# Turning the second half of a normalised input by DMA in a two-layer graph kernel

## The chip, the cores and the metric

The kernel runs on one core of a Trainium2 chip. The metric is device time in microseconds (us) of one execution. Engines are called PE (TensorE, matrix products), DVE (VectorE), ACT (ScalarE), POOL (GpSimd) and SP (SyncE, which here issues every DMA, in one queue and in program order). Each engine works through its own instructions in order and waits for others by semaphores.

## The reference, cut to what matters

The input x has 128 elements of 128 nodes by 512 features. Layer 0 is a graph convolution; layer 1 is masked attention of eight heads. Both begin with a layer normalisation and a ReLU, and both add their result to x.

```
# layer 0
h = relu(layernorm(x))
x = x + norm_adj @ (h @ weight) + bias
# layer 1
h = relu(layernorm(x))
q, k, v = h @ Wq + bq, h @ Wk + bk, h @ Wv + bv        # 8 heads of 64
attn = softmax(q k^T / 8 + (1 - adj) * -1e9)
x = x + (attn v) @ Wo + bo
```

The change concerns the h of layer 1: it stands node by feature after the normalisation and is needed feature by node, as operand of the three products q, k and v.

## The kernel before, in words

**Groups and stages.** The 128 elements are worked in 32 groups of four (`GB = 4`, `NG = 32`). A stage t has five blocks: W (layer 0's product for group t+1), Q, K and V (the three projections of group t), Y (the output projection of group t-1). Each block has seven steps, `W0` to `W6` and so on, one for each of seven block products in a Strassen-like scheme (`PRODUCTS`, lines 31 to 39), split once more inside; the sums of operands that the scheme needs are made on POOL (`combine`, `combine_one`), and DVE and ACT add the products from the accumulator banks into the result (`add` at line 440, `read` at 455, the copies at 770 and 784). PE's order is thus fixed: P1, P5, P2, P6, P3, P7, P4 in every block.

**The plan.** All other work is put between the steps by hand: `at(t, "V2", f, ...)` runs f just before step V2 of stage t, "V2b" comes after the step's matmuls and first reads, and "V2c" after the rest. Nothing is reordered afterwards, so the place of a call is its place in the queue of each engine that it uses, SP's queue too.

**The normalised input of layer 1 (h).** For group g = t+1, `norm_h(g, b)` (line 715, an activation at 344) makes h of element b in a tile of a pool of two. Elements 0 and 1 go by DMA: `split_h` (736) copies the fp32 words on ACT into two planes of 16 bits, in an attention buffer that is free at the time; after element 1 the planes are written to DRAM (743) and `turn_h` (745) reads them back with a transposing DMA (748) into the first eight slots of `op_norm`, blocks A11 and A12. Elements 2 and 3 go by PE: `transpose_h` (719) makes sixteen 64-row transposes for each into a bank (730), and ACT copies the bank into blocks S1 and A22 (731). Both are in stage t: `norm_h` at V1, V2, V5, V6; `split_h` at V2b and V3, `turn_h` at Y0, `transpose_h` at Y1 and Y2. `attention_operands` at Y5 starts POOL's sums over all four blocks (373 to 376, then 94); Q of the next stage reads them.

**The attention planes** go the same way as elements 0 and 1 of h: `split_att` (850) writes planes (854), `turn_att` (856) reads them back transposed (857), for elements 0 to 3 of the group before; elements 2 and 3 are needed by `attend` at V0.

**Other transfers in SP's queue.** x of group t+2 is loaded in two halves (`load_x`, 170): the first half at W2 into a buffer that a store (897) must first have left, the second at W5, just behind `turn_att` of element 0. `ln1` needs the second half at Q3b: DVE takes its statistics (325), and behind them in DVE's order stand reads of Q's banks. Four of the five weights stream through two buffers, each in four parts of 11, 11, 11 and 7 slots (`PARTS`, `reload_w`, 1063): `reloads_of` (1065) lists the places, and in its row "W" the V weights come at W6, Q4, Q1 and K3; the part of Q4 holds W22 and T3, which V4 and V5 read.

Of the kernel before, what the change touches and what calls it, by code (L numbers as in the profile page):

```python
# [9 lines left out]
U16 = mybir.dt.uint16  # L10
# [17 lines left out]
A11, A12, S1, A22, S2, S3, S4 = range(7)  # L28
# [17 lines left out]
LEFT_AT = {A11: 0, A12: 4, S1: 8, A22: 12, S2: 16, S3: 20, S4: 24}  # L46
# [51 lines left out]
def kernel(  # L98
# [16 lines left out]
    nc = tc.nc  # L115
    B, N, D = x.shape
    P = 128
    H = 8
    HD = D // H
    NC = D // P  # L120
    GB = 4
    NG = B // GB
# [4 lines left out]
    dp = ctx.enter_context(tc.tile_pool(name="dp", bufs=1, space=bass.MemoryType.DRAM))  # L127
# [27 lines left out]


    planes_dram = [dp.tile([P, 2, H * P], U16, tag=f"planes_{b}", name=f"planes_{b}") for b in range(GB)]
    h_dram = dp.tile([P, 2, H * P], U16, tag="planes_h", name="planes_h")
    adj_sb, an = (att_buf[2][:, i, :] for i in range(2))
    bias_part = att_buf[4][:, 0:NC, :].rearrange("p c f -> p (c f)")  # L160
    ones = att_buf[4][:, NC, :]
# [222 lines left out]
    op_mix, op_norm, op_att = (Operands(f"op_{k}") for k in "aho")  # L384
# [250 lines left out]
    hs = {}  # L635
# [83 lines left out]
    def transpose_h(g, b):  # L719
# [13 lines left out]
            pt.bitcast(U16).rearrange("p (z c n) -> p c n z", z=2, c=NC),  # L733
        )

    def split_h(g, b):


        h2 = hs.pop((g, b)).bitcast(U16).rearrange("n (c f z) -> n z c f", c=NC, z=2)
        planes = att_of(g - 1, -1).bitcast(U16).rearrange("n h k -> n (h k)")  # L740
        nc.scalar.copy(planes.rearrange("n (z c j f) -> n z c j f", z=2, c=NC, j=2)[:, :, :, b, :], h2)
        if b == 1:
            nc.sync.dma_start(h_dram, planes.rearrange("n (z f) -> n z f", z=2))

    def turn_h(g):
        op_h[g] = op_norm
        blocks = op_norm.t.bitcast(U16)[:, LEFT_AT[A11] : LEFT_AT[A11] + 8, :]
        nc.sync.dma_start_transpose(out=blocks, in_=h_dram.rearrange("n z f -> (n z) f"))

    def attention_operands(g):  # L750
        op_h[g].combine(nc.vector if g < 2 else nc.gpsimd, g > 0, within=nc.gpsimd)
# [5 lines left out]
    qs, ks, vs = {}, {}, {}  # L757
# [36 lines left out]
    def att_of(g, b):  # L794


        return att_buf[(b - g) % (GB + 1)]
# [106 lines left out]
    def at(slot, place, f, *args):  # L904
        plan.setdefault((slot, place), []).append((f, *args))

    for t in range(-1, NG + 1):
# [3 lines left out]
        if 0 <= t - 1 < NG - 1:  # L911
            g = t - 1
# [27 lines left out]
        if t == 0:  # L940

            at(0, "Q0b", ln2, 1, 0)
            at(0, "Q1b", ln2, 1, 1)
            at(0, "K6", norm_h, 1, 0)
            at(0, "K6", norm_h, 1, 1)
            at(1, "W0", transpose_h, 1, 0)
            at(1, "W0", norm_h, 1, 2)
            at(1, "W1", transpose_h, 1, 1)
            at(1, "W1", norm_h, 1, 3)
            at(1, "W2", transpose_h, 1, 2)  # L950
            at(1, "W3", transpose_h, 1, 3)
            at(1, "W4b", attention_operands, 1)
            at(2, "Q5", attention_residual, 1, 0)
            at(2, "K1", attention_residual, 1, 1)
        elif 1 <= t + 1 < NG and t >= 0:
            g = t + 1
            at(t, "K0b" if g < NG - 1 else "Q0b", ln2, g, 0)
            at(t, "K6b" if g < NG - 1 else "Q3b", ln2, g, 1)
            if g == NG - 1:

                places = ("Q3", "Q4", "Q5", "Q5", "Q6", "Q6", "K1", "K2", "K2")
                steps = ((norm_h, 0), (norm_h, 1), (transpose_h, 0), (norm_h, 2), (transpose_h, 1), (norm_h, 3))
                steps += ((transpose_h, 2), (transpose_h, 3))
            else:
                places = ("V1", "V2", "V2b", "V3", "V5", "V6", "Y1", "Y2", "Y5")
                steps = ((norm_h, 0), (norm_h, 1), (split_h, 0), (split_h, 1), (norm_h, 2), (norm_h, 3))
                steps += ((transpose_h, 2), (transpose_h, 3))
                at(t, "Y0", turn_h, g)
            for place, (f, b) in zip(places, steps):
                at(t, place, f, g, b)  # L970
            at(t, places[8], attention_operands, g)
            at(t + 1, "Q3", attention_residual, g, 0)
            at(t + 1, "Q4", attention_residual, g, 1)
# [6 lines left out]
        if 2 <= t + 2 < NG:  # L980
            g = t + 2
# [4 lines left out]
            places = (("Q3", "Q5"), ("Q4", "Q6"), ("Q5b", "K1"), ("Q6", "K2"))  # L986
# [6 lines left out]
        if 0 <= t < NG:  # L993
            g = t
            for b in (0, 1, 3, 2):
                at(t, "V0", scores, g, b)
            if t > 0:
                at(t, "V0", output_operands, t - 1)
            at(t, "V1b", row_max, g, 0)
            at(t, "V3b", exponentials, g, 0, 0, H // 2)  # L1000
            at(t, "V4b", exponentials, g, 0, H // 2, H)
            at(t, "V6", softmax_end, g, 0)
            if last:
                at(t, "V5b", row_max, g, 1)
                at(t, "V5b", exponentials, g, 1, 0, H // 2)
                at(t, "V6", exponentials, g, 1, H // 2, H)
                at(t, "Y1b", softmax_end, g, 1)
                at(t, "Y2", transpose_att, g, 0)
                at(t, "Y4", transpose_att, g, 1)
            else:  # L1010
                if t > 0:
                    at(t, "V3b", row_max, g, 1)
                    at(t, "Y1", exponentials, g, 1, 0, H // 2)
                    at(t, "Y2", exponentials, g, 1, H // 2, H)
                    at(t, "Y4", softmax_end, g, 1)
                else:
                    at(t, "V4b", row_max, g, 1)
                    at(t, "V5b", exponentials, g, 1, 0, H // 2)
                    at(t, "V6", exponentials, g, 1, H // 2, H)
                    at(t + 1, "W1b", softmax_end, g, 1)  # L1020
                at(*((t, "Y3b") if t > 0 else (1, "W1")), split_att, g, 0)
                at(t, "V6b", row_max, g, 2)
                at(*((t, "Y1") if t > 0 else (1, "W0")), add_mask, g, 3)
                at(*((t, "Y3b" if g == NG - 2 else "Y6b") if t > 0 else (1, "W4b")), row_max, g, 3)
        if last:
            g = t
# [38 lines left out]
    def reloads_of(t):  # L1065

        when = {
            "W": ((t, "W6"), (t, "Q4"), (t, "Q1"), (t, "K3")),
            "Q": ((t, "K4"), (t, "K6"), (t, "V0"), (t, "V1")),
            "V": ((t, "V3"), (t, "Y0"), (t, "Y1"), (t, "Y3")),  # L1070
            "Y": ((t, "Y5"), (t + 1, "W0"), (t + 1, "W0"), (t + 1, "W3" if t + 1 < NG - 1 else "Q5")),
        }
        if t == 1:

            when["Q"] = ((1, "K3"),) * 4
        for kind in "WQVY":
            if kind == "W" and t + 1 == NG or kind in "QV" and t == NG:
                continue
            reading[0] += 1
            for part, place in enumerate(when[kind]):  # L1080
                at(*place, reload_w, reading[0] + 2, part)
# [89 lines left out]
    with tc.manual_schedule(  # L1171
        engines={
            mybir.EngineType.PE,
            mybir.EngineType.DVE,
            mybir.EngineType.Activation,
            mybir.EngineType.Pool,
            mybir.EngineType.SP,
        }
    ):
        prologue()  # L1180
        for t in range(1, NG + 1):
            reloads_of(t)

        for t in range(NG + 1):
            if t > 0:
                block(t, "W", t + 1, gcn_weight)
            if t < NG:
                block(t, "Q", t, lambda g: qk(g, 0))
                block(t, "K", t, lambda g: qk(g, 1))
                block(t, "V", t, values)  # L1190
            block(t, "Y", t - 1, attention_out)
            if 0 < t < NG:
                store_half(t - 1, 0)
            elif t == NG:
                store_half(t - 1, 1, slice(0, 256))
# [41 lines left out]
```

## Time and profile before

| what | value |
|---|---|
| three timed executions | 2237.06, 2238.38 and 2242.81 us, median 2238.38 |
| the profiled execution's own time | 2240.26 us, of it 2238.5 us span |
| busy in the span | PE 2218.4 us, POOL 1867.5, DVE 1799.0, ACT 1387.1 |
| DMA | 565.15 MB in 448,697 packets; 326,352 packets under 512 B |
| issues | 150 transposing DMAs (121 of attention, 29 of h), 121 + 29 writes of planes, 484 weight parts and a few more |
| granted PE clock | 0.999 |

From one stage's first score matmul to the next it is 68.27 us in most stages from 2 to 28, and up to 70.17 in the others. All times "in the stage" below are counted from that first score matmul, which is in step V0; the blocks then follow as V, Y, W, Q, K. A profile of the chip is read here as lists of the instructions of each engine in order of time; a bracket at the end of a line tells how long the engine stood idle before that instruction and what ended it.

### The profile page before, as it was taken

Reading aid. Unit: us, or ns where it says so; the run is one execution under the profiler, and the core shown is the slowest. Engines: PE = TensorE matmul, PEld = TensorE weight load, DVE = VectorE, ACT = ScalarE, POOL = GpSimd, SP = SyncE. Lnnn points to the kernel's source line nnn. Section 1 sums busy time; section 2 is a strip of 40 time slices with the busy share of each in tenths; the row PEclk is TensorE's granted clock in tenths of the full one; section 3 lists DMA queues with packets and bytes.
Section 4 is the critical chain, followed back from the end, with each engine's and each line's share of the span. In section 5 each row is a group of like instructions: output and inputs, shape, how many; then the busy total and the mean of one; then the engine's idle time right before and its main releaser. Section 6 shows DMA issues by size and latency. Waiting matters only on the chain.

```text
span 2238.5 us, 79241 instructions
## 1 busy us (share of the span) xinstructions
PE 2218.4 (99%) x32679; PEld 1905.3 (85%) x32679; DVE 1799.0 (80%) x4371; ACT 1387.1 (62%) x3556; POOL 1867.5 (83%) x1928
## 2 busy tenths in 40 slices
PE   9999999999999999999999999999999999999999
PEld 7688888888888888888888888888888888888887
DVE  7777888878888788887788877888878888888876
ACT  4565666656657556666566565566665666655754
POOL 6899889888898888988888987889888889888864
PEclk9999999999999999999999999999999999999999
DMA  5388999899988899988998999988888988899982
GB/s 168 155 267 253 283 252 269 249 254 286 261 247 259 250 282 262 265 270 245 256 292 251 252 255 248 296 252 256 254 256 266 275 269 261 252 258 291 244 242 93
DMA packets 448697, 565.15 MB, mean 252 GB/s; under 512 B 326352, under 2 KB 333648, under 8 KB 447824
## 3 DMA queue, kind: packets, MB, share of 16 engines
q1 hardware_dynamic: 448336, 560.08, 86.0%
q8 instruction: 258, 4.23, 0.8%
q14 instruction: 103, 0.84, 0.1%
HBM read 358.68 MB, written 122.68 MB: 215 GB/s over the span
## 4 chain that ended last, share of the span: by engine, by line
PE 89%; SPq 4%; DVE 2%; DMA 2%; POOL 2%; ACT 1%; issue 1%; POOLq 0%; DVEq 0%
PE bank_a L140 33%; PE bank_d L140 20%; PE bank_b L140 10%; PE bank_c L140 10%; PE pa L140 4%; SPq L857 3%; PE bank_d L813 3%; PE po L879 2%; DMA xt<-in_x_dram 2%; PE pt L730 1%; PE pss L813 1%; PE bank_b L879 1%; PE bank_a L879 1%; PE bank_b L813 1%; DVE st L325 1%
## 5 line engine op out<-in xcount | busy, mean ns | idle before, releaser
L840 ACT ACTIVATE att<-att,nmx 128x128 f32<-128x128 f32 x1024 | 396.4, 392 | 0.5 <-DMA w<-in_L_gnn_Wo_dram 0.5
L140 PE MATMUL bank_a<-op_h,w 128*64 128x256 f32 x2976 | 352.8, 379 | 0.0
L440 DVE TENSOR_TENSOR xt<-xt,bank_d 128x512 f32<-128x512 f32 x610 | 269.9, 467 | 11.4 <-PE bank_d L140 0.5
L140 PEld LDWEIGHTS bank_a<-op_h,w 128*64 128x64 f32 x2976 | 207.5, 137 | 81.3 <-issue 0.2
L853 ACT COPY att<-att 128x2048 uint16<-128x2048 uint16 x121 | 229.3, 1895 | 65.1 <-POOL att L848 65.1
L848 POOL TENSOR_TENSOR att<-att,rsm 128x1024 f32<-128x1024 f32 x128 | 241.9, 1899 | 31.1 <-DVE rsm L847 31.0
L344 ACT ACTIVATE h<-xt,nb,rs 128x512 f32<-128x512 f32 x254 | 207.4, 818 | 94.8 <-POOL nb L333 93.1
L331 POOL TENSOR_TENSOR rs<-ve,mhalf 128x2 f32<-128x2 f32 (+1 forms) x129 | 92.0, 713 | 184.3 <-DVE ve L330 183.7
L325 DVE BATCH_NORM_STATS2 st<-xt 128x6 f32<-128x512 f32 x256 | 173.2, 676 | 67.3 <-DMA xt<-in_x_dram 67.3
L140 PE MATMUL bank_d<-op_h,w 128*64 128x128 f32 (+1 forms) x3424 | 222.0, 275 | 0.6 <-DVE q L440 0.5
L94 POOL TENSOR_TENSOR op_o<-op_o 128x256 f32<-128x256 f32 x297 | 210.9, 735 | 10.0
L94 POOL TENSOR_TENSOR op_a<-op_a 128x256 f32<-128x256 f32 x279 | 197.5, 732 | 14.4 <-DVE op_a L376 4.8
L770 ACT ACTIVATE q<-bank_a,bqk 128x256 f32<-128x256 f32 x192 | 80.0, 467 | 199.8 <-PE bank_a L140 199.8
L140 PEld LDWEIGHTS bank_d<-op_h,w 128*64 128x64 f32 x3424 | 194.6, 137 | 8.9 <-DVE q L440 2.2
L94 POOL TENSOR_TENSOR op_h<-op_h 128x256 f32<-128x256 f32 x270 | 191.4, 733 | 12.4 <-DVE op_h L376 3.1
L840 ACT ACTIVATION_READ_ACCUMULATOR att<-att,nmx 128x1 f32 x1024 | 195.3, 191 | 0.0
L140 PE MATMUL bank_a<-w,op_o 128*64 128x256 f32 x1536 | 182.1, 379 | 0.0
L140 PE MATMUL bank_a<-w,op_h 128*64 128x256 f32 x1488 | 177.9, 381 | 0.0
L140 PE MATMUL bank_a<-w,op_a 128*64 128x256 f32 x1488 | 176.4, 379 | 0.0
L455 DVE TENSOR_TENSOR xt<-bank_a,xt 128x512 f32<-128x512 f32 x252 | 166.7, 682 | 3.3 <-PE bank_a L140 2.9
L832 DVE TENSOR_REDUCE nmx<-att 128x8 f32<-128x1024 f32 x128 | 154.9, 1210 | 0.0
L348 POOL TENSOR_TENSOR xt<-xt,b 128x1024 f32<-128x1024 f32 (+1 forms) x65 | 153.0, 2357 | 0.0
(183 smaller groups left out, 5664.4 us busy)
## 6 DMA issues: line engine op xcount, KB each, us to landing
w<-wd_v SPq DMA_DIRECT2D x93, 704.0 KB, 5.9
w<-wd_o SPq DMA_DIRECT2D x93, 704.0 KB, 7.2
w<-wd_q SPq DMA_DIRECT2D x90, 704.0 KB, 6.8
planes<-att SPq DMA_DIRECT2D x121, 512.0 KB, 6.5
w<-wd SPq DMA_DIRECT2D x87, 704.0 KB, 5.7
xt<-in_x_dram SPq DMA_DIRECT2D x63, 512.0 KB, 6.6
out_dram<-xt SPq DMA_DIRECT2D x62, 512.0 KB, 4.9
planes_h<-att SPq DMA_DIRECT2D x29, 512.0 KB, 3.0
```

Source lines behind the costliest of these rows:

```text
L94: engine.tensor_tensor(twice(out), twice(x), twice(y), ALU.subtract if minus else ALU.add)
L140: nc.tensor.matmul(out[y : y + P // 2], lhsT[:, y : y + P // 2], rhs, **flags)
L325: nc.vector.bn_stats(self.st[:, j, :], self.src[:, j, :])
L344: nc.scalar.activation(h, src[:, j, :], AF.Relu, bias=nb[:, j : j + 1], scale=rs[:, j : j + 1])
L348: nc.gpsimd.tensor_tensor(t, t, bias.unsqueeze(1).to_broadcast([P, t.shape[1], D]), ALU.add)
L440: nc.vector.tensor_tensor(dst, dst, src, f)
L455: nc.vector.tensor_tensor(t, src.rearrange("p (r f) -> p r f", r=2), t, ALU.add)
L813: nc.tensor.matmul(pss[p][:, c, :], qs[g][rows, c, cols], ks[g][rows, c, cols], start=True, stop=True)
L832: nc.vector.tensor_reduce(nmx, att_of(g, b), AX.X, ALU.max, negate=True)
L840: nc.scalar.activation(att[:, h, :], att[:, h, :], AF.Exp, bias=nmx[:, h : h + 1], scale=1.0, accum_out=sm[:, h : h + 1])
L848: nc.gpsimd.tensor_tensor(att, att, rsm.unsqueeze(2).to_broadcast([P, H, P]), ALU.mult)
L853: nc.scalar.copy(planes, halves)
```

## The change

All four elements of h now go through DRAM. The planes are made in q's tile, whose contents the scores have just used, one half of it for each pair of elements, with a DRAM tile for each pair. The first pair is normalised at K6 and split right behind the scores at V0. The second pair is normalised at V0b and V1, split at V1b and V2. The writes stand at V1b and V2b, the transposing reads at V5 and Y1b. `transpose_h` remains for groups 0, 1 and the last alone, so 29 groups change. One part of the V weights moves from Q4 to K3.

```diff
-    h_dram = dp.tile([P, 2, H * P], U16, tag="planes_h", name="planes_h")
+    h_dram = [dp.tile([P, 2, H * P], U16, tag=f"planes_h_{y}", name=f"planes_h_{y}") for y in range(2)]
...
+    def h_planes(g, half):
+        t = qs[g - 1][:, 2 * half : 2 * half + 2, :].bitcast(U16)
+        return t.rearrange("n c f -> n (c f)")
+
     def split_h(g, b):
+        half, j = divmod(b, 2)
         h2 = hs.pop((g, b)).bitcast(U16).rearrange("n (c f z) -> n z c f", c=NC, z=2)
-        planes = att_of(g - 1, -1).bitcast(U16).rearrange("n h k -> n (h k)")
-        nc.scalar.copy(planes.rearrange("n (z c j f) -> n z c j f", z=2, c=NC, j=2)[:, :, :, b, :], h2)
-        if b == 1:
-            nc.sync.dma_start(h_dram, planes.rearrange("n (z f) -> n z f", z=2))
+        planes = h_planes(g, half).rearrange("n (z c j f) -> n z c j f", z=2, c=NC, j=2)
+        nc.scalar.copy(planes[:, :, :, j, :], h2)
+
+    def write_h(g, half):
+        nc.sync.dma_start(h_dram[half], h_planes(g, half).rearrange("n (z f) -> n z f", z=2))
 
-    def turn_h(g):
+    def turn_h(g, half):
         op_h[g] = op_norm
-        blocks = op_norm.t.bitcast(U16)[:, LEFT_AT[A11] : LEFT_AT[A11] + 8, :]
-        nc.sync.dma_start_transpose(out=blocks, in_=h_dram.rearrange("n z f -> (n z) f"))
+        first = LEFT_AT[S1 if half else A11]
+        blocks = op_norm.t.bitcast(U16)[:, first : first + 8, :]
+        nc.sync.dma_start_transpose(out=blocks, in_=h_dram[half].rearrange("n z f -> (n z) f"))
...
-                places = ("V1", "V2", "V2b", "V3", "V5", "V6", "Y1", "Y2", "Y5")
-                steps = ((norm_h, 0), (norm_h, 1), (split_h, 0), (split_h, 1), (norm_h, 2), (norm_h, 3))
-                steps += ((transpose_h, 2), (transpose_h, 3))
-                at(t, "Y0", turn_h, g)
+                places = ("K6", "K6", "V0b", "V1", "V1b", "V2", None, None, "Y5")
+                steps = ((norm_h, 0), (norm_h, 1), (norm_h, 2), (norm_h, 3), (split_h, 2), (split_h, 3))
+                for half in range(2):
+                    at(t, ("V1b", "V2b")[half], write_h, g, half)
+                    at(t, ("V5", "Y1b")[half], turn_h, g, half)
...
                 at(t, "V0", output_operands, t - 1)
+                for b in range(2 if t < NG - 2 else 0):
+                    at(t, "V0", split_h, t + 1, b)
...
-            "W": ((t, "W6"), (t, "Q4"), (t, "Q1"), (t, "K3")),
+            "W": ((t, "W6"), (t, "K3"), (t, "Q1"), (t, "K3")),
```

## The prediction

> **What bounds the kernel now.** I read the page's busy shares first, then the waits, then one stage in order of time, with PE, DVE and SP side by side.
>
> ```profile
> PE 2218.4 (99%) x32679; PEld 1905.3 (85%) x32679; DVE 1799.0 (80%) x4371; ACT 1387.1 (62%) x3556; POOL 1867.5 (83%) x1928
> ...
> DMA  5388999899988899988998999988888988899982
> ...
> q1 hardware_dynamic: 448336, 560.08, 86.0%
> ```
>
> Two things are nearly full: PE, and in the steady part the sixteen DMA engines (8 and 9 tenths). The change moves work from the first to the second, so the question is which wait of PE ends at a DMA. The waits over the whole span:
>
> ```profile
> DVE st L325 <- DMA xt<-in_x_dram: 67.3, 51, 3.0
> ...
> PE bank_b L140 <- DVE q L440: 4.9, 7, 1.2
> ```
>
> ```profile
> SPq L743 <- ACT att L741: 394.0, 29, 15.8
> ```
>
> The second of these is of SP's own queue. Only DVE waits for a transfer in a way that reaches PE, for x of group t+2. And SP's queue stands 394.0/29 = 13.6 us a stage before the write of h, for ACT's split. Stage 14 in order of time shows the chain:
>
> ```profile
> 1069.87 9.44 SPq L857 DMA_TRANSPOSE att<-planes  x1
> ...
> 1079.37 0.57 SPq L170 DMA_DIRECT2D xt<-in_x_dram  x1
> ...
> 1084.64 0.69 DVE L325 BATCH_NORM_STATS2 st<-xt 128x6 f32<-128x512 f32 x1 [2.75 <-DMA xt<-in_x_dram]
> ...
> 1087.59 0.44 PE L140 MATMUL bank_b<-op_h,w 128*64 128x128 f32 x4 [0.95 <-DVE q L440]
> ```
>
> A transposing read holds SP until the engines have worked off what is ahead of it (9.44 us); the second half of x is issued behind it, lands late, and DVE stands before it in order, so PE waits for a bank. I took the landing of that half in stages 2 to 28 from the landing records (counted from the stage's first score matmul, as all stage times here): mean 46.83, from 45.58 to 48.77. In all 27 stages the stage's length is 68.27 + max(0, landing - 46.87), to 0.01 us. So PE's own floor is 68.27, the deadline for x is 46.87, and lateness now costs 9.6 us in the 27 stages together.
>
> **The change part by part.**
>
> *PE transposes removed.* Sixteen matmuls for each of two elements:
>
> ```profile
> 1052.43 0.61 PE L730 MATMUL pt<-ident,h 128*64 128x128 bf16 x16
> 1052.88 1.05 PE L140 MATMUL bank_d<-w,op_o 128*64 128x128 f32 x16
> ```
>
> From the first of them to the next product is 0.447 us (median of 70 sets). Two a stage, 29 stages: -25.9 us, all of it on PE's path. The floor becomes 68.27 - 0.89 = 67.38, and since the places lie before Q, the deadline for x becomes 45.98.
>
> *ACT.* Two copies from the bank fall away, two splits come, at the same price:
>
> ```profile
> L731 ACT COPY op_h<-pt 128x1024 uint16<-128x1024 uint16 x66 | 66.1, 1003 | 27.7 <-PE pt L730 27.7
> ...
> L741 ACT COPY att<-h 128x1024 uint16<-128x1024 uint16 x58 | 57.5, 1043 | 0.0
> ```
>
> The two normalisations at K6 (0.82 us each) fall into an idle 2.67 us before the copies of `attend`; were that cover gone, they would delay these by up to 1.6 us. Order matters in V. In stage 14 ACT is free of the scores at 1040.25; two splits (0.94 apart), the first copy of V (0.48), two normalisations (0.71 each) and the third split come before the copy of bank_d into v, which moves from 1043.21 to 1044.97. DVE's four sums from bank_d, queued behind it, move from 1044.82 to about 1045.6, and the third of them would end near 1046.65, where PE wants the bank at 1046.36: 0.3 us a stage, at most 0.5, nothing if the sums run closer. This raises the floor to 67.68, but is not added to lateness of x, whose deadline moves with it.
>
> *DMA added.* One write of planes and one transposing read a stage. From the packet records: the 307,200 packets of 256 bytes took 8586 us for 150 transposing reads, 3.58 us of all sixteen engines each; writes of planes 3300 us for 150, 1.38 each. The steady stage holds 5.9 us without any transfer (mean of stages 7 to 27, from about 5 to 11 us), because SP waits for the split at V2b. The first write now goes at 6.0 into that hole, so it costs nothing; without the hole it would cost 1.4. The second write goes at 10.3, as the only one did at 10.2.
>
> The rest is a walk along the queue by median landings of stages 7 to 27. Before: weight part 16.0, h 18.5, weight parts 21.3, 23.5 and 24.9, planes 27.0 (waited for ACT until 23.66), weight part 29.7, store 31.4 (waited for DVE until 27.46), x 46.5. After: the first h read is issued early but behind the same part, so 18.5 stays; the second is queued behind the parts of 21.4 and 23.6. A transposing read adds 2.45 to 3.12 to the landings (five places), so it lands near 26.2, and the last part at 27.6. The planes, now ready at about 20.4 since ACT is free earlier, land near 29.0, the weight part at 31.1, the store at 32.7: 1.3 later than before, the rest absorbed where the queue had waited for ACT and DVE. After the store nothing waits for the engines, so the queue hands +1.3 to x.
>
> Against this walk stands a row: in the five stages in which that last weight part landed after 26, x landed at 46.36 on average, 0.47 earlier than the mean of all; the latest, at 27.2, gave 47.2, +0.4. So lateness there has been swallowed so far. Bounds of the shift of x: -0.5 from those five, +2.6 if a whole transposing step reaches it. I take +0.85, half way between the walk and the stage nearest to it.
>
> The page "DMA: Bandwidth & Descriptors" of the Trainium skill (section "Latency and other measured facts") gives a transposing DMA 261 GB/s with a non-contiguous middle dimension, which for 512 KB would be an estimated 2.0 us; the rows here say 2.45 to 3.12. By the page the shift would be about 0.6 smaller and the sum about 13 us lower; the rows decide. The same page (section "Alternative transpose paths") calls TensorE the useful path for data already on chip, which speaks against this change; the row for it is PE's 0.45 us against 5 us of DMA time.
>
> *The weight part moved.* 704 KB leave the place before the reads of planes 2 and 3 (a step of 2.09) and follow them. These reads land at 62.0 and 64.6, PE needs them at 64.7 and 65.5: without the move the +1.3 would break that; with it there is more room than before. The part is read at V4, some 10 us into the next stage, and lands near 67: free.
>
> *POOL.* It starts h's sums at 25.6 and now waits for the second read, 26.2. The 0.6 us vanish in the 2.26 us that POOL stands idle before the next `ln1`.
>
> **Sum.** With each stage at max(67.38, landing + 0.85 + 21.40), lateness over the 27 stages is 45.9 us instead of 9.6: -25.9 + 36.3 = +10.4. The same sum gives -11.6 with no shift (-9.3 with the ACT floor), 0 at +0.45, +38.7 at +1.9. Profiled 2240.26 + 10.4 = 2250.7; the median lies 1.9 below the profiled execution, so 2249.
>
> **The rivals.**
> - *The queue swallows the added read* (33%). The five late stages speak for it, the walk against it. With a shift of -0.5 to 0 the sum is -20.7 to -9: 2218 to 2229, most likely 2225. Faster.
> - *It comes out even* (15%): a shift of 0.2 to 0.7, between 2232 and 2245. Nothing new happens, PE's gain is paid back at Q3b.
> - *Nothing is absorbed* (5%): shift 2.6, +57.6, 2296. Against it: at 24 and 28 us in stage 10 only 10.5 and 13.5 packets are in flight, where a full queue keeps sixteen.
> - *Late operands* (5%): the second read lands after 29.5, 4 us past POOL's start, beyond what lies between the sums on S1 (ready 34.7) and their use at Q1 (38.8). Each us beyond costs 27 us; at 30.5 about 2276. It has the weight part at V3 and two more ahead of it, yet some 3 us of room.
> - *PE isn't the bound*, so its transposes were free: then -25.9 is void and it ends near 2275. The 0.01 us fit of the stage length with DVE at 80% speaks against it; its chance is in the forecast's tail.
>
> The forecast, a shift of 0.7 to 2, has 42%. This measurement can tell about 0.3%, 6.7 us. Faster 0.33, same 0.15, slower 0.52. The range goes from 2218 (shift -0.5) to 2277 (shift 1.9).
>
> **What would show it.** Right: no 16-packs of L730 in the steady stages; DVE's wait for x several times 67.3 us; SP's wait for the split down from 13.6 us a stage to a few; stage lengths of 67.4 or a little above where x lands before 46, and growing one for one with its landing. The shift of x is the decisive number: at 47.7 on average I am right, below 46.8 wrong. A PE gap near 10 us in the stage behind DVE's sums on v would show the ACT order. POOL waiting for the second read for over 4 us would show late operands.

## The result, and the profile after

The changed kernel takes 2236.35 us (median of 16 runs, 2233.1 to 2243.0), the kernel before 2237.70 beside it (16 runs). The ratio is 0.9995, 95% interval 0.9986 to 1.0004: no change that can be measured. The forecast was 2249, slower; the case "it comes out even" had 15%.

The page of the changed kernel, busy shares, DMA by slices and SP's queue:

```profile
PE 2205.3 (99%) x31751; PEld 1881.0 (84%) x31751; DVE 1800.5 (81%) x4371; ACT 1385.4 (62%) x3556; POOL 1867.9 (84%) x1928
...
DMA  5489999999999999999999999999999999999982
...
q1 hardware_dynamic: 512832, 590.50, 90.4%
```

PE has lost 928 instructions and 13.1 us of busy time, and the DMA slices have gone from a mix of 8 and 9 tenths to 9 throughout. The work did move. The profiled execution took 2238.29 us (2236.5 of span), 1.97 less than the one of before. The waits of the engines (total us, times, longest):

```profile
DVE st L325 <- DMA xt<-in_x_dram: 95.1, 57, 3.4
...
PEld bank_d L140 <- DVE v L440: 11.9, 29, 0.8
...
PEld bank_b L140 <- DVE q L440: 8.6, 13, 1.8
PEld bank_c L140 <- DVE xt L440: 7.6, 10, 1.6
POOL op_h L373 <- DMA op_h<-planes_h: 7.1, 15, 0.9
```

DVE's wait for x rose from 67.3 to 95.1 us. The second line is new: 29 waits, one in each changed stage, for DVE's sums on v. PE now also waits for bank_c in ten places (7.6 us; before in six, 1.7 us); that wait stands behind DVE's sums for x and hangs on the *first* half of x. POOL waits for the second read of h 0.5 us at a time. The waits of SP's queue:

```profile
SPq L748 <- ACT q L745: 373.0, 58, 10.8
...
SPq L170 <- DMA out_dram<-xt: 94.7, 28, 5.6
```

SP waits as long as before for ACT's splits, 373.0/29 = 12.9 us a stage against 13.6, only ahead of two writes instead of one. And the first half of x waits longer for the store that must first leave its buffer: 94.7 us instead of 40.7. The store is late, as forecast. The line of the kernel before:

```profile
SPq L170 <- DMA out_dram<-xt: 40.7, 27, 3.3
```

**The stage as a maximum.** With both traces at hand, the length of a stage can be written as the largest of four numbers, counted from its first score matmul: PE's own floor (the length when no input is late); landing of x's first half + 27.83; landing of its second half + 21.40; landing of the attention planes of element 3 + 2.91. This fits all 27 stages of before to 0.01 us, and of after 26 of 27 to 0.05 us; stage 4 is 0.30 longer. In after the second half of x comes last in 16 stages, the planes of element 3 in four, the first half in two. What the two kernels differ in (stages 2 to 28):

```
                                              before     after   forecast
PE floor                                       68.27     67.75      67.68
second half of x lands, mean                   46.83     47.01      47.68
stages longer than the floor                       9        23
their lateness over the floor, summed           9.6      21.4       45.9 (over 67.38)
27 stages together                            1853.0    1850.7
```

The floor gives 27 * 0.523 = 14.1 us, the lateness takes 11.8 of it back.

Two places of stage 14 (it begins at 1038.34) show both losses. First V, with ACT, DVE and PE in order of time, in the changed kernel:

```profile
1046.08 1.05 ACT L745 COPY q<-h 128x1024 uint16<-128x1024 uint16 x1
...
1047.01 0.60 ACT L790 COPY v<-bank_d 128x512 f32<-128x512 f32 x1
...
1047.64 1.54 DVE L440 TENSOR_TENSOR v<-v,bank_d 128x256 f32<-128x256 f32 x4 [0.64 <-ACT v L790]
...
1048.78 1.75 PE L140 MATMUL bank_d<-w,op_h 128*64 128x128 f32 x28 [0.16 <-DVE v L440]
```

The same place in the kernel before (its stage 14 begins at 1036.25), where neither DVE nor PE stood idle:

```profile
1043.21 0.57 ACT L784 COPY v<-bank_d 128x512 f32<-128x512 f32 x1
...
1044.82 1.53 DVE L440 TENSOR_TENSOR v<-v,bank_d 128x256 f32<-128x256 f32 x4
...
1046.36 1.70 PE L140 MATMUL bank_d<-w,op_h 128*64 128x128 f32 x28
```

In the changed kernel a split of the second pair stands ahead of ACT's copy of bank_d into v; DVE's sums wait 0.64 us for that copy, and PE then 0.16 us for the bank, 10.4 us into the stage. Then the end of the queue's chain, in Q of the same stage:

```profile
1074.87 7.68 SPq L863 DMA_TRANSPOSE att<-planes  x1
...
1082.60 0.57 SPq L170 DMA_DIRECT2D xt<-in_x_dram  x1
...
1087.38 0.69 DVE L325 BATCH_NORM_STATS2 st<-xt 128x6 f32<-128x512 f32 x1 [3.37 <-DMA xt<-in_x_dram]
...
1090.32 0.44 PE L140 MATMUL bank_b<-op_h,w 128*64 128x128 f32 x4 [1.57 <-DVE q L440]
```

This is the chain of before, here in the longest of the 27 stages: x lands at 49.02, the stage takes 49.02 + 21.40 = 70.42.

### The profile page after: what moved, and what is told of

Same layout as the page of the kernel before. It is cut to its first block, busy times and chain, and to the rows that moved or that the text cites. A ratio compares the mean times of both kernels' runs of the same rounds, so it can differ in the third digit from the quotient of the medians.

```text
span 2236.5 us, 77530 instructions
## 1 busy us (share of the span) xinstructions
PE 2205.3 (99%) x31751; PEld 1881.0 (84%) x31751; DVE 1800.5 (81%) x4371; ACT 1385.4 (62%) x3556; POOL 1867.9 (84%) x1928
## 4 chain that ended last, share of the span: by engine, by line
PE 54%; POOL 21%; DVE 9%; DMA 6%; ACT 5%; SPq 3%; issue 3%; DVEq 0%; POOLq 0%
PE bank_a L140 20%; PE bank_d L140 14%; POOL op_a L94 7%; PE bank_c L140 7%; PE bank_b L140 6%; PE pa L140 4%; DMA xt<-in_x_dram 4%; SPq L863 3%; DVE v L440 3%; DVE xt L440 2%; DMA out_dram<-xt 2%; ACT q L745 2%; POOL op_a L376 1%; POOL op_a L374 1%; POOL op_a L373 1%
## 5 line engine op out<-in xcount | busy, mean ns | idle before, releaser
L344 ACT ACTIVATE h<-xt,nb,rs 128x512 f32<-128x512 f32 x254 | 201.3, 818 | 104.5 <-POOL nb L333 102.8
L325 DVE BATCH_NORM_STATS2 st<-xt 128x6 f32<-128x512 f32 x256 | 173.7, 678 | 95.1 <-DMA xt<-in_x_dram 95.1
L846 ACT ACTIVATION_READ_ACCUMULATOR att<-att,nmx 128x1 f32 x1024 | 203.9, 199 | 0.0
L94 POOL TENSOR_TENSOR op_h<-op_h 128x256 f32<-128x256 f32 x270 | 191.4, 733 | 12.5 <-DVE op_h L376 3.1
```

Source lines behind the costliest of these rows:

```text
L94: engine.tensor_tensor(twice(out), twice(x), twice(y), ALU.subtract if minus else ALU.add)
L325: nc.vector.bn_stats(self.st[:, j, :], self.src[:, j, :])
L344: nc.scalar.activation(h, src[:, j, :], AF.Relu, bias=nb[:, j : j + 1], scale=rs[:, j : j + 1])
L846: nc.scalar.activation(att[:, h, :], att[:, h, :], AF.Exp, bias=nmx[:, h : h + 1], scale=1.0, accum_out=sm[:, h : h + 1])
```

## The experiments

All times are medians; "floor", "x" (the mean landing of its second half in stages 2 to 28) and "sum" (the 27 stages together) are read from one profiled execution each. That execution lay 6.3 us above the median in a_part_behind and 4.3 in b_best, 5.5 below it in b_extra_w, and within 2.6 in the others, so counts of late stages are those of one execution. The names below are those of the records.

```
                    us    before   ratio   95% interval      floor      x     sum
b_no_pe          2210.76  2237.32  0.9883  0.9870 - 0.9897   67.38  45.65  1824.5
a_no_second      2218.84  2236.57  0.9923  0.9908 - 0.9938   67.75  45.84  1829.7
a_act_order      2229.85  2237.32  0.9965  0.9953 - 0.9978   67.38  46.71  1843.5
b_extra_y        2250.12  2237.66  1.0057  1.0043 - 1.0070   68.27  47.34  1861.3
b_extra_w        2296.78  2237.66  1.0267  1.0251 - 1.0283   68.27  48.86  1904.5
a_part_behind    2230.93  2237.32  0.9975  0.9966 - 0.9983   67.75  45.97  1849.6
b_part_behind    2234.92  2237.32  0.9994  0.9985 - 1.0003   68.27  45.21  1846.6
a_weight_back    2238.70  2236.57  1.0007  0.9998 - 1.0017   67.75  46.79  1849.3
a_best           2220.31  2237.66  0.9924  0.9912 - 0.9937   67.38  45.60  1834.4
b_best           2234.50  2237.66  0.9987  0.9978 - 0.9996   68.27  45.57  1849.6
a_best2          2215.56  2236.57  0.9910  0.9894 - 0.9927   67.38  45.63  1827.8
```

(In b_extra_w every stage was late, so that its shortest is 69.30; the floor of before is entered.)

### The transposes alone taken out (b_no_pe)

```diff
-                at(t, place, f, g, b)
+                if f is not transpose_h or g == NG - 1:
+                    at(t, place, f, g, b)
```

> The kernel before without the PE transposes of elements 2 and 3 and without ACT's copies of them in groups 2 to 30 (left out: these two elements are not turned, their blocks hold old data). No DMA is added. Theory D: PE's floor falls to 67.38, the deadline of x moves as well, so lateness of x rises and the time falls by about 10 to 12 us, not by the 25.9 us that the transposes take. Rival N (the transposes lay beside other work): no gain. Rival P (PE alone sets the time): the full 25.9.

With the transposes go ACT's copies of their banks, so elements 2 and 3 aren't turned and their blocks hold old data. Measured: -26.6 us, floor 67.38. The expected 10 to 12 us were missed: lateness was to rise from 9.6 us and fell to 5.3. The floor is what PE's share of the prediction said (67.38, 25.9 us in 29 stages). That the time fell by nearly those 25.9 us, as rival P has it, is in part luck: the profile's 27 stages lost 28.5, of it 24.2 by the floor and 4.3 by lateness. What no expectation said: x lands 1.18 us earlier, at 45.65, though no transfer was added or removed. The waits of this kernel:

```profile
DVE st L325 <- DMA xt<-in_x_dram: 54.9, 49, 2.7
```

DVE waits less for x (54.9 against 67.3), although its deadline is earlier. The medians of the queue (stages 2 to 27) show where the time comes from: the planes that SP writes for ACT are issued at 20.96 instead of 23.66, the store that it issues for DVE at 26.57 instead of 27.46, and the store lands at 30.24 instead of 31.40. Without the transposes PE, and behind it ACT and DVE, come to these places earlier.

### The second pair's transfers alone taken out (a_no_second)

```diff
-                for half in range(2):
+                for half in range(1):
```

> The changed kernel without the write and the transposing read of the second pair (left out: elements 2 and 3 are not turned, their blocks hold old data; the splits stay). Theory S (slack at the store, gates of ACT and DVE about 1 us earlier): x's second half lands near 45.8 us in the stage instead of 47.0, the stages stand at the floor of 67.75 that ACT's order sets, and the time falls to about 2216 to 2222. My first reading, that the added read hands 1.3 us and more to x, would be the same size here, so this run tells how large the push is that the earlier gates had to cover. Theory F: little change, since 704 KB of weights a stage keep the engines full.

The splits of the second pair stay; its blocks hold old data. Measured: 2218.84, x at 45.84, as expected. The waits:

```profile
DVE st L325 <- DMA xt<-in_x_dram: 46.0, 45, 2.8
...
PEld bank_d L140 <- DVE v L440: 11.7, 29, 0.8
```

The lateness is gone (under 1 us in 27 stages), while PE's wait behind the sums on v stays as it is: two separate losses. The three kernels make a ledger against before. Transposes gone: -26.6. With ACT's new order, the second pair's splits, the first pair's new places and the moved weight part: -17.7, so these cost 8.9 (27 * 0.37 = 10.0 by the floors). With the second pair's write and read as well: -1.3, so these cost 16.4. x is later by 47.01 - 45.84 = 1.17 us.

### ACT's order put right (a_act_order)

```diff
-                places = ("K6", "K6", "V0b", "V1", "V1b", "V2", None, None, "Y5")
+                places = ("K6", "K6", "V0b", "V1", "V1c", "V2", None, None, "Y5")
```

> The changed kernel with the split of element 2 placed behind ACT's copy of bank_d into v (V1c instead of V1b). Theory D: PE's gap at 10.4 us in the stage (0.15 us in the bank_d products, the floor 0.37 above 67.38) goes, but stages with late x keep their length, so the sum falls by only 1 to 3 us, although the floor falls by 10 us over 27 stages. Rival G (the ACT order is what ate the gain): the time falls by the whole 10 us.

Measured: 6.5 us less than the changed kernel; the floor is 67.38. The waits:

```profile
DVE v L440 <- ACT v L790: 7.7, 30, 0.3
...
PEld bank_b L140 <- DVE q L440: 10.9, 14, 1.4
```

The split now stands behind the copy. DVE's wait for that copy falls from 26.8 to 7.7 us, its value before the change, and PE's wait on bank_d behind v is gone from the list. The line of the kernel before:

```profile
DVE v L440 <- ACT v L784: 7.7, 30, 0.3
```

The gain lies between the two expectations: D (1 to 3 us) put it too low, G (10 us) too high: in the stages that x ends, the lower floor gains nothing, and the wait on bank_b grew from 8.6 to 10.9.

### The same bytes ahead of the store, and behind it (b_extra_y, b_extra_w)

Into the kernel before comes one plain write of 1 MB a stage, of data that nobody reads. Once it stands at Y1b, the place of the second read of h, once at W1, behind the store.

```diff
+    spare_dram = dp.tile([P, 16, P], F32, tag="spare", name="spare")
...
+    def extra():
+        nc.sync.dma_start(spare_dram, w_buf[2][:, 0:16, :])
...
+                at(t, "Y1b", extra)
```

> The kernel before with one more DMA a stage: 1 MB of constant weights written from SBUF to an unused DRAM tile, issued at Y1b, the place of the added transposing read (nothing reads it). About 2.5 us of all sixteen engines. Theory S (queue slack at the store): a transfer added ahead of the planes and the store is swallowed there; the second half of x lands at most 0.5 us later than 46.83 and the time rises by at most 7 us. Theory Q (my walk: the queue hands lateness on): x lands 1.3 to 2.5 us later and the time rises by 24 to 57 us.

> The same extra write, issued at W1, behind the store and two weight parts. Theory S: there is no slack behind the store other than the slow steps of a short queue, so x lands 1 to 2.5 us later, clearly more than with the write at Y1b, and the time rises by 15 to 57 us. Theory F (only the total of DMA work counts): the same time as with the write at Y1b, within 4 us.

Measured: +12.5 us at Y1b (at most 7 was expected), +59.1 us at W1 (15 to 57). The waits, first of the write at Y1b, then of the one at W1 (the added line makes L325 L326 here):

```profile
DVE st L326 <- DMA xt<-in_x_dram: 92.4, 58, 3.4
```

```profile
DVE st L326 <- DMA xt<-in_x_dram: 141.9, 58, 4.5
...
PEld bank_c L140 <- DVE xt L441: 42.4, 28, 2.9
```

The same 1 MB delays x by 0.51 us in the one place and by 2.03 in the other, where the first half is late too (28 waits on bank_c). The two kernels differ in that place alone. So F, that only the bytes count, falls, and "swallowed" is true of what stands ahead of the store, not of all. It is not swallowed whole there, as the 12.5 us show.

Where it goes is seen from the landings of the store and of x's second half (medians of stages 2 to 27):

```
                  store issued   store lands   x lands   between
before                   27.46         31.40     46.75     15.35
b_no_pe                  26.57         30.24     45.58     15.34
a_no_second              26.94         30.27     45.85     15.58
after                    26.94         33.01     46.86     13.85
b_extra_y                27.46         33.09     47.42     14.33
b_extra_w                27.46         31.27     48.79     17.52
```

Where the store lands 3.3 to 3.9 us after its issue, the way from it to x is 15.3 to 15.6 us. Where the queue is behind, and the store lands about 6 us after its issue (after, b_extra_y), the same transfers take 1.0 to 1.5 us less. (The 17.52 of b_extra_w holds the extra write's own step of 2.55.) Step by step, from landing to landing, nearly all of the difference stands in one place: the weight part right behind the store adds 2.10 us on average in after and 3.35 before; the seven steps from there to the second half of x add up to 11.9 and 12.0. Between 30 and 34 us of the stage, in stretches where weight parts are moved, the sixteen engines move 383 to 407 GB/s after, 255 to 270 before, with 16.6 and 15.0 packets in flight. The 5632-byte packets of the weight parts take 236 ns there on average in after and 323 before. What else is in flight beside them doesn't explain it: from 32 to 34 us in before it is nearly nothing but weight parts (310 ns), and so it is from 20 to 24 us, where the same packets take 216 to 221 ns. The trace doesn't say why these packets run faster; that they do is in the records.

### One weight part placed behind x (a_part_behind, b_part_behind)

The last part of q's weights stands behind the first half of x and ahead of the second. It goes behind the second, in the changed kernel and in the one before alike:

```diff
-            "Y": ((t, "Y5"), (t + 1, "W0"), (t + 1, "W0"), (t + 1, "W3" if t + 1 < NG - 1 else "Q5")),
+            "Y": ((t, "Y5"), (t + 1, "W0"), (t + 1, "W0"), (t + 1, "W5" if t + 1 < NG - 1 else "Q5")),
```

> The changed kernel with the last part of the q weights (448 KB, a step of 1.1 us in the landings) issued behind the second half of x instead of ahead of it. Theory D (deadline): a stage of the changed kernel lasts max(67.75, landing of x's second half + 21.40) us, and lateness of x holds 21.4 us of the removed transposes' gain. The landing goes from 47.0 to about 45.9 us in the stage, and the time falls by about 15 us (0.993 of before). Theory F (DMA engines full): the same bytes move, so what x gains another transfer loses; the time stays within 4 us of the changed kernel.

> The same edit in the kernel before. Theory D: the landing of x goes from 46.8 to about 45.7 us, but its floor is 68.27 and its lateness only 9.6 us, so the time falls by about 8 us (0.9965), half of what it does in the changed kernel. Theory F: no change.

Measured: 5.4 us less than the changed kernel where 15 was expected; 2.4 less than before where 8 was. The second half lands 1.04 us earlier, as expected, and limits one stage instead of 16. The first half lands as in the changed kernel (40.26 against 40.09) and now limits 12 stages; the planes of element 3 limit four. These counts are of an execution 6.3 us above the median, so they show which deadlines come next rather than how much each costs. The expectation moved one deadline and left the other two out.

### The weight part of the change put back (a_weight_back)

```diff
-            "W": ((t, "W6"), (t, "K3"), (t, "Q1"), (t, "K3")),
+            "W": ((t, "W6"), (t, "Q4"), (t, "Q1"), (t, "K3")),
```

> The changed kernel with the part of the V weights back at Q4. Theory M: it stands behind x in the queue, so x lands as in the changed kernel, but planes of element 3 land about 2 us later (from 64.2 to 66) and pass their deadline (stage end minus 2.91) in most stages: the time rises by 15 to 40 us. Rival: the part's place is of no account, within 4 us.

Measured: 2238.7, and 1849.3 in the 27 stages against 1850.7. The expected loss of 15 us or more didn't come; the intervals of the two kernels overlap. The planes of element 3 limit nine stages instead of four (3.3 us together over the other terms, instead of 1.4), and x lands 0.2 earlier. Of the change's parts this one is worth nothing that can be told.

### All places put right (a_best, b_best, a_best2)

a_best has ACT's new order and two parts of q's weights placed later; b_best has these two places in the kernel before. a_best2 adds one V part:

```diff
-            "W": ((t, "W6"), (t, "K3"), (t, "Q1"), (t, "K3")),
+            "W": ((t, "W6"), (t, "K3"), (t, "K3"), (t, "K3")),
...
-            "Y": ((t, "Y5"), (t + 1, "W0"), (t + 1, "W0"), (t + 1, "W3" if t + 1 < NG - 1 else "Q5")),
+            "Y": ((t, "Y5"), (t + 1, "W3" if t + 1 < NG - 1 else "W0"), (t + 1, "W0"), (t + 1, "W5" if t + 1 < NG - 1 else "Q5")),
```

> The changed kernel with three moves: the split of element 2 behind ACT's copy of bank_d (V1c), the q weights' second-issued part (W22 and T3) from W0 to W3, behind the first half of x, and their last part behind the second half of x (W5). Theory M (several deadlines): in the profiles so far a stage lasts max(floor, first half of x + 27.83, second half of x + 21.40, planes of element 3 + 2.91) us, each landing counted in the stage; the change raised the landings while the gates of ACT and DVE came earlier. Here the floor is 67.38, the first half lands near 38 (deadline 39.55), the second near 45.6 (deadline 45.98): the time falls to about 2214 to 2218 (0.990 to 0.9915 of before). Theory F (DMA engines full, 90% over the span): what is moved ahead pushes the planes of element 3 past their deadline and the time stays at 2228 to 2231, as for the single moves.

> The same two moves of q's weight parts in the kernel before (it has no ACT order to mend). Theory M: the floor stays 68.27 and only its 9.6 us of lateness can go: 2229 to 2233 (0.996 to 0.998). The difference to the changed kernel with the same moves, some 15 us, is then what the change is worth once the transfers meet their deadlines. Theory F: the two differ by less than 4 us.

> The best version so far with one more part of the V weights (W21 and T2) moved from Q1 to K3, behind the planes of elements 2 and 3. In that version's profile 5 of 27 stages end with the planes of element 3 at their limit, 2.91 us ahead of the next stage, and that costs some 4 us. Theory M: these stages are relieved, 2215 to 2219. Rival: the planes wait for ACT's copies instead, no change within 2 us.

Measured: 2220.31, 2234.50 and 2215.56, the last within its range. a_best and b_best both miss their ranges, by 2 and 1.5 us: in five stages of each the planes of element 3 came last. Between them lie 14.2 us, about the 15 expected. The V part of a_best2 stood ahead of those planes; moved, no stage is limited by them. Its page and its waits:

```profile
span 2213.9 us, 77475 instructions
```

```profile
DVE v L440 <- PE bank_b L140: 58.1, 32, 1.9
...
DVE st L325 <- DMA xt<-in_x_dram: 39.6, 36, 3.3
```

DVE's wait for x is less than half of that of the changed kernel (95.1). Fourteen of 27 stages stand at the floor of 67.38. In six x still comes last, and seven exceed all four terms, by 0.03 to 0.77 us, six of them with a PE wait on bank_d behind DVE's sums on q at 44 to 45 us; what is late there wasn't followed up. It beats the kernel before by 0.9% (0.9910, 0.9894 to 0.9927), and the changed kernel's median lies 20.8 us above its own.

## Why the prediction was wrong, and where it was right

**Right: PE and ACT.** The transposes are worth 25.9 by the working; without them the floor falls to the 67.38 that it named, and the time by 26.6 (b_no_pe, where less lateness is in the number too). The wait by ACT's order is where it was put, in front of the same bank 10.4 us into the stage, and its size 0.37 us where 0.3 was taken and 0.5 was the bound. Also right is that it and the lateness of x don't add: the distance from x to the stage's end is 21.40 with the floor at 68.27, 67.75 and 67.38.

**Right: the queue up to the store.** Forecast and measured landings: first write in the hole (8.60), second read 26.2 and 26.41, last weight part 27.6 and 27.80, planes 29.0 and 29.29, weight part 31.1 and 31.75, store 32.7 and 33.01. POOL was not hit: 7.1 us of waiting for the second read, spread over 15 stages.

By the 261 GB/s (non-contiguous middle dimension) of the Trainium skill's page "DMA: Bandwidth & Descriptors" (section "Latency and other measured facts") the second read would have added an estimated 2.0 us; it added 2.88. A shift smaller by 0.6, as by the page, gives a sum lower by 16 us in the working's own formula, where it says 13. That forecast, 2233 to 2236, would have been near the result by luck: the read took longer than the page's figure, not less.

**Wrong: "After the store nothing waits for the engines, so the queue hands +1.3 to x."** This is the step that failed. The store came 1.61 us later (median), x 0.18 (mean). The way from store to x shrank from 15.35 to 13.85. The walk had taken it as a fixed sum of steps. In the profiles the step of the weight part right behind the store shrank from 3.35 to 2.10 us (means); b_extra_y and b_extra_w show that it isn't fixed: of the same bytes ahead of the store 0.51 us arrives at x, behind it 2.03. The row that stood against the walk, the five stages with a late weight part and an early x, was telling this, and halving between the two left a term of 0.85 that measured 0.18. By the sign that the prediction set itself (47.7 right, below 46.8 wrong) the mean landing of 47.01 lies between, nearer to wrong; DVE's wait for x grew 1.4 times, not several times.

**Not in the working: what x would have done without the added transfers.** The 0.18 is not their price. In b_no_pe and a_no_second x lands at 45.65 and 45.84, because with PE's transposes gone the store's gate on DVE comes earlier too; the working moved the deadline of x by 0.89 and knew of an earlier gate only for the planes. Against a_no_second the second pair makes the store 2.74 us later (33.01 against 30.27), of which 1.17 arrive at x, and costs 16.4 us. So the change could have given 17.7 and not, as the working's bound for "no shift" has it, 11.6.

**Wrong: "without the move the +1.3 would break that".** The moved weight part is worth nothing that can be told (a_weight_back): without it the planes of element 3 come last in nine of 27 stages, and the time is the same. Nor was there "more room than before" in every stage: those planes limit four stages after and none before.

**Wrong: SP's wait for the split, from 13.6 us a stage "to a few".** It is 12.9. The first write ends its wait at 5.97 instead of 10.20, but the second stands at 10.24, and the weight part behind it goes at 10.67, as it did at 10.63. The hole was filled with one write, not closed.

**The rival that came out, and why.** "It comes out even" asked for a shift of 0.2 to 0.7, paid at Q3b. The shift is 0.18, just below. By the working's own formula (floor 67.68, landings of before + 0.18) the 27 stages would be 4.2 us shorter; with the floor as measured (67.75) and the second halves as they landed, 4.4. The profile has 2.35. Of the remaining 2.0, 1.6 are paid in the four stages where the planes of element 3 came last, 0.1 in the two where the first half of x did, and 0.3 in stage 4, which none of the four numbers covers. No rival named these. So the case was right in its outcome and in its main place, Q3b. PE's 24.1 us in these stages went to ACT's order (10.0 by the floor) and to lateness (11.8).

The page's section "Alternative transpose paths", which calls TensorE useful when data is already on chip, was weighed against this change. As first placed, nothing was gained by leaving TensorE. With ACT's order and two weight parts placed anew, turning by DMA was worth 14.2 us (a_best against b_best), and a_best2 is 21 us below the kernel before, of which places alone give about 3 (b_best). Whether the change pays was decided by where the transfers stood.

## What to carry to other kernels

Write a stage as the maximum of its deadlines, each fitted from the trace, and carry all of them through a forecast: moving one without the next (the first half of x, the planes) overstated the gain of a_part_behind and b_part_behind, and by a little that of a_best. When work leaves the bounding engine, the gates that it sets for the DMA queue move too, so work out the landings again and not the deadline alone. Before handing a delay on along a queue, look for places where it waits for an engine, and ask in which of them a transfer added ahead is swallowed; of the 1 MB added here ahead of the store x paid 0.51 us, of that added behind it 2.03.

## What was not expected of the hardware

The time that a transfer adds to the queue depends on what is queued before it: a 704 KB weight part added 3.35 us on average behind a store that landed 3.9 us after its issue, and 2.10 us where the store was queued behind other transfers and landed 6.1 us after it, at 255 to 270 and 383 to 407 GB/s, with 15.0 and 16.6 packets in flight. Packets in flight differ by a tenth only, the rates by half, so the number in flight hardly told a queue with room from a full one. The cause of the different rates wasn't tried.
